# Attention woven step by step into the projections, with 8 slots for stacked heads and 2 for probabilities

## The chip, the core and the metric

The kernel runs on one core of one Trainium2 chip. The metric is the device time of one execution in microseconds (us), as the median of several runs. A core has five engines that run side by side and wait for one another through semaphores: TensorE (PE: matrix products and transposes into PSUM), VectorE (DVE), ScalarE (ACT), GpSimd (POOL) and SyncE (SP), whose queue issues all DMA transfers here. Each engine works through its own instructions in a fixed order.

## What is computed

Two transformer layers over 8 batches of 256 tokens of width 512, in float32. The first is a block with self-attention, cross-attention and an MLP; the second is a recurrent time-mix and channel-mix block, which the change leaves alone. The attention of the first layer, cut to what matters:

```python
def attention(q, k, v, mask):                       # 16 heads of width 32
    scores = einsum('bhqd,bhkd->bhqk', q, k) / sqrt(32)
    scores = scores * mask - 10000.0 * (1.0 - mask)
    return einsum('bhqk,bhkd->bhqd', softmax(scores), v)

h = layernorm(x);  q, k, v = split(h @ w_qkv + b_qkv)
x = x + merge(attention(q, k, v, mask1)) @ w_ao + b_ao
h = layernorm(x);  q = h @ w_q + b_q;  k, v = split(ctx @ w_kv + b_kv)
x = x + merge(attention(q, k, v, mask2)) @ w_co + b_co
x = x + gelu(layernorm(x) @ w1 + b1) @ w2 + b2
```

## The kernel before

**Precision.** Every projection is done on operands that are split into a high and a low part; `mm3` (lines 232 to 234) makes three matmuls of each product. A projection unit of one batch is 48 matmuls of 256 columns for Q or K (`proj_t`, four output quarters of 12 matmuls, in two PSUM banks) or 24 of 512 columns for V and for the output (`proj_n`, two halves of 12).

**Stages of a batch.** The list `jobs` holds 8 batches of self-attention, then 8 of cross-attention, then the MLP. Each job has four stages. Stage `a` loads the input, normalises it (DVE, with a power on GpSimd), transposes it on PE and splits it (ACT, and GpSimd at line 275). Stage `b` makes Q, K and V, and `stack` lays the heads out anew: for each of four groups `hm` it fills a Q tile and a K tile with four DMAs each (line 385), 32 DMAs a batch, in the ring `stk` of six slots. In such a tile the high and low parts of a head lie below each other, so that one matmul makes the whole product of a head. Stage `c` is the attention, stage `d` the output projection and the residual sum (line 348), stored by DMA.

**One head in `attend`.** Two matmuls make the scores `sc` (line 404, two banks). DVE multiplies them by the scaled mask into `e` (line 406, four slots) and takes row minima with the mask's offset (line 408, twice). ACT makes exponentials and their sums (line 411, twice). PE transposes the result with four transposes into `tr` (line 415, two banks), ACT copies it to `pt` (line 419, four slots of two heads). After four heads, eight small products with V fill `cx` (line 424, two banks). After eight heads the reciprocals of the sums are transposed and spread over the partitions (lines 433 to 448), and the context is normalised and split into `ch` and `cl` (lines 449 to 453).

**What sets the order.** The Python loop records stages in the order `c(i)`, `d(i-1)`, `b(i+1)`, `a(i+2)`; this order gives each instruction its priority. A scheduler then puts the instructions of every engine into a fixed order when the program is built, by priority among what it takes to be ready, with a model of its own of how long things take. `tc.high_priority` raises an instruction's priority, and `tc.issue_after(x)` keeps an instruction behind `x` on its engine. Tiles live in named slots of SBUF (`SLOTS`) and PSUM (`BANKS`); a tile that takes a slot waits until the last use of the slot's tile before. Weights, MLP and time-mix follow behind the attention with priorities that are written out by hand (`SEQ`, `AT`).

Of the kernel before, what the change touches and what calls it, by code (L numbers as in the profile page):

```python
# [39 lines left out]
def slots(text):  # L40

    r = {}
    for item in text.split():
# [11 lines left out]
    "attn": slots(  # L55
        "x:a0,a1 xr:a2 y:a3 u:a4-a7 s:a8-a11 v:a12,a13 ch:a14 cl:a15 stk:a16-a21 "
        "w:a16-a23 w1:d1,d3 e:b0-b3 pt:a22-a25 rb:b9 mc:d0,d1 mn:d2,d3 row:b8 sums:c0 mx:c1 rs_:c2 rsp:c3 cp:c4,c6"
    ),
# [47 lines left out]
def block_kernel(ctx: ExitStack, tc: tile.TileContext, a: dict, out: bass.AP):  # L106
# [120 lines left out]

    latest = [None]

    def mm3(o, ah, al, bh, bl, first, last):  # L230
# [77 lines left out]
    def proj_t(w, xt, emit, kind="o", noc=4, pairs=False):  # L308

        (wh, wl), (xh, xl) = w, xt  # L310
        for o2 in range(noc // 2):
            o = bank(kind, [P, 2, T])
            for oo in range(2):
                oc = 2 * o2 + oo
                cs = slice(oc * P, (oc + 1) * P)
                for k in range(KC):
                    mm3(o[:, oo, :], wh[:, k, cs], wl[:, k, cs], xh[:, k, :], xl[:, k, :], k == 0, k == KC - 1)
                if not pairs:
                    emit(oc, o[:, oo, :])
            if pairs:  # L320
                emit(slice(2 * o2, 2 * o2 + 2), o)

    def proj_n(ws, xts, emit, kind="o"):

        for t in range(2):
            ts = slice(t * P, (t + 1) * P)
            o = bank(kind, [P, D])
            n = len(ws)
            for u in range(n):
                (wh, wl), (xh, xl) = ws[u], xts[u]  # L330
                for k in range(KC):
                    mm3(o, xh[:, k, ts], xl[:, k, ts], wh[:, k, :], wl[:, k, :], u == 0 and k == 0, u == n - 1 and k == KC - 1)
            emit(t, o)

# [54 lines left out]
    def attend(qs, ks, v, mc, mn, cp):  # L389
# [3 lines left out]
        lo = wt("cl", [P, KC, T], F32R)  # L393
        for h2 in range(2):
            cx = bank("cx", [P, 2, T])
            sums = wt("sums", [P, 2, 4, 2])
            mx = wt("mx", [P, 2, 4, 2])
            for kk2 in range(2):
                hm = 2 * h2 + kk2
                pts = []  # L400
                for hc in range(4):
                    sc = bank("sc", [P, 2, T])
                    for t in range(2):
                        TE.matmul(sc[:, t, :], qs[hm][:, hc, t * P : (t + 1) * P], ks[hm][:, hc, :], start=True, stop=True)  # L404
                    e = wt("e", [P, 2, T])
                    V.tensor_tensor(e, sc, mc, ALU.mult)  # L406
                    for t in range(2):
                        V.tensor_tensor_reduce(e[:, t, :], e[:, t, :], mn[:, t, :], 1.0, 3.0e38, ALU.add, ALU.min, accum_out=mx[:, kk2, hc, t : t + 1])  # L408
                    pr = e
                    for t in range(2):  # L410
                        S.activation(pr[:, t, :], e[:, t, :], AF.Exp, bias=mx[:, kk2, hc, t : t + 1], scale=-1.0, accum_out=sums[:, kk2, hc, t : t + 1])  # L411
                    pt_ps = bank("tr", [P, 2, T])
                    for kk in range(2):
                        for t in range(2):
                            TE.transpose(pt_ps[:, kk, t * P : (t + 1) * P], pr[:, t, kk * P : (kk + 1) * P], ident)  # L415
                    if hc % 2 == 0:
                        ptt = wt("pt", [P, 2, 2, T])
                    pt = ptt[:, hc % 2]
                    S.copy(pt, pt_ps)  # L419
                    pts.append(pt)  # L420

                def product(kk, hc):
                    h = 4 * hc + hm
                    return TE.matmul(cx[32 * hc : 32 * hc + 32, kk2, :], v[:, kk, 32 * h : 32 * h + 32], pts[hc][:, kk, :], start=kk == 0, stop=kk == 1)  # L424

                with tc.high_priority(1000):
                    first = product(0, 3)
                    with tc.issue_after(first.ins):
                        for kk in range(2):
                            for hc in range(4 if kk else 3):  # L430
                                product(kk, hc)
            rs_ = wt("rs_", [P, 2, 4, 2])
# [3 lines left out]
            V.tensor_copy(rsp[:, :, :, 0, :], rs3)  # L436
            V.tensor_tensor(rsp[:, :, :, 1, :], rs3, r32(rsp[:, :, :, 0, :]), ALU.subtract)
            rt_ps = bank("tr", [8, 2, T])
            for kk in range(2):
                for t in range(2):  # L440
                    TE.transpose(rt_ps[:, kk, t * P : (t + 1) * P].bitcast(F32R), rsp[:, t, kk].rearrange("p u m -> p (u m)"), identr)
            rt = wt("e", [8, 2, T], F32R)
            S.copy(rt, rt_ps)
            rb_ps = bank("tr", [P, 2, T])
            for kk in range(2):
                TE.matmul(rb_ps[:, kk, :], pick, rt[:, kk, :], start=True, stop=True)
            cn = wt("rb", [P, 2, T])
            S.copy(cn, rb_ps)
            V.tensor_tensor(cn, cx, cn, ALU.mult)
            for kk in range(2):  # L450
                k = 2 * h2 + kk
                S.activation(hi[:, k, :], cn[:, kk, :], AF.Identity, bias=cp[:, k : k + 1])
                V.scalar_tensor_tensor(lo[:, k, :], cn[:, kk, :], cp[:, k : k + 1], r32(hi[:, k, :]), ALU.add, ALU.subtract)
        return hi, lo

# [10 lines left out]
    class SelfAttention:  # L466
# [9 lines left out]

        def b(self, b, xt):
            q = qk_t(W[0, "q"], xt, "bqkv", 0)
            k = qk_t(W[0, "k"], xt, "bqkv", 4)
# [3 lines left out]
        def c(self, b, got):  # L483
# [3 lines left out]
            s, v = got  # L487
            return attend(*s, v, *W["mask"], W[0, "cp"])

# [7 lines left out]
    class CrossAttention:  # L497
        slots = "attn"

        def a(self, b, _):  # L500
            if b == 0:
                W[1, "k"] = load_unit(a["wkv"][:, 0:D], "w1")
                W[1, "v"] = load_unit(a["wkv"][:, D : 2 * D], "w1")
                W[1, "q"] = load_unit(a["wq"], "w1")
            et = split_t(load_x(a["ctx"][b], "x"), "u")
            return et, ln_t(load_x(x1[b], "x"), "ln2s", "ln2b")

        def b(self, b, got):
            et, xt = got
            mask = mask_terms(a["cmask"][b, 0])  # L510
            k = qk_t(W[1, "k"], et, "bkv", 0)
            v = v_n(W[1, "v"], et)
            q = qk_t(W[1, "q"], xt, "bq", 0)
            return mask, stack(q, k), v

        def c(self, b, got):
# [3 lines left out]
            mask, s, v = got  # L520
            return attend(*s, v, *mask, W[1, "cp"])

# [549 lines left out]
    def run(ph, stage, b, key):  # L1072
        phase[0] = ph.slots
        got[key] = getattr(ph, stage)(b, got.get(key))


    seq = SEQ.split()
# [19 lines left out]
    for i in range(-2, len(jobs) + 1):  # L1097
        for stage, j in (("c", i), ("d", i - 1), ("b", i + 1), ("a", i + 2)):
            if 0 <= j < len(jobs):
                ph, b = jobs[j]  # L1100
                run(ph, stage, b, j)
        if i >= len(jobs) - 2:
# [54 lines left out]
```

## Time and profile before

| | us |
|---|---|
| median of 3 runs | 1851.51 |
| lowest and highest run | 1848.45, 1852.3 |
| the profiled execution | 1852.05 |
| its span | 1850.1 |
| PE, DVE, ACT, POOL busy in the span | 1691.5, 1313.8, 1152.7, 722.1 |
| first and last scores (line 404) | 53.5, 787.6 |

The profile is one execution. Busy time of PE counts a matmul from its start to its modelled end, and matmuls overlap, so a busy PE is not PE at its peak; the distance between the starts of matmuls tells their price. The granted clock is the share of full speed that PE was given in a stretch. A wait is shown with who ended it, its total, how many there were and the longest.

### The profile page before, as it was taken

Reading aid. Unit: us, or ns where it says so; the run is one execution under the profiler, and the core shown is the slowest. Engines: PE = TensorE matmul, PEld = TensorE weight load, DVE = VectorE, ACT = ScalarE, POOL = GpSimd, SP = SyncE. Lnnn points to the kernel's source line nnn. Section 1 sums busy time; section 2 is a strip of 40 time slices with the busy share of each in tenths; the row PEclk is TensorE's granted clock in tenths of the full one; section 3 lists DMA queues with packets and bytes.
Section 4 is the critical chain, followed back from the end, with each engine's and each line's share of the span. In section 5 each row is a group of like instructions: output and inputs, shape, how many; then the busy total and the mean of one; then the engine's idle time right before and its main releaser. Section 6 shows DMA issues by size and latency. Waiting matters only on the chain.

```text
span 1850.1 us, 38996 instructions
## 1 busy us (share of the span) xinstructions
PE 1691.5 (91%) x14576; PEld 1416.9 (77%) x14576; DVE 1313.8 (71%) x3065; ACT 1152.7 (62%) x2848; POOL 722.1 (39%) x494
## 2 busy tenths in 40 slices
PE   4999999989999999889999999989899998988997
PEld 3777777777778787679999877768788776767876
DVE  4777767787787868864632768876676778799774
ACT  3777777778687868884544454636636453745643
POOL 2011111122222212122211049999999549997000
PEclk9999999999999999999999999999999899889999
DMA  6655545455655655889643555597675848954431
GB/s 188 154 130 127 124 119 130 125 166 150 158 143 143 154 131 139 263 298 330 219 159 107 204 186 165 136 286 222 189 253 172 237 122 254 318 183 141 125 112 48
DMA packets 261026, 324.45 MB, mean 175 GB/s; under 512 B 159155, under 2 KB 162107, under 8 KB 260838
## 3 DMA queue, kind: packets, MB, share of 16 engines
q1 hardware_dynamic: 260838, 321.96, 58.9%
q8 instruction: 116, 1.90, 0.4%
q14 instruction: 72, 0.59, 0.1%
HBM read 156.98 MB, written 97.78 MB: 138 GB/s over the span
## 4 chain that ended last, share of the span: by engine, by line
PE 59%; DVE 15%; DMA 8%; ACT 7%; POOL 5%; issue 4%; SPq 2%; DVEq 0%; ACTq 0%; POOLq 0%
PE o L232 8%; PE o L233 7%; PE o L234 7%; PE mm L232 5%; PE mm L233 5%; PE mm L234 5%; PE tr L415 4%; PE cx L424 3%; PE sc L404 2%; POOL X L848 2%; DVE e L408 2%; DVE e L406 2%; PE out L234 2%; PE out L232 2%; PE out L233 2%
## 5 line engine op out<-in xcount | busy, mean ns | idle before, releaser
L411 ACT ACTIVATE e<-e,mx 128x256 f32<-128x256 f32 x512 | 256.9, 506 | 42.7 <-DVE mx L408 42.1
L406 DVE TENSOR_TENSOR e<-sc,mc 128x512 f32<-128x512 f32 x256 | 171.6, 681 | 99.2 <-PE sc L404 52.7
L408 DVE CUSTOM_DVE_ANT_0 e<-e,mn 128x256 f32<-128x256 f32 x512 | 222.3, 475 | 1.0
L848 POOL TENSOR_TENSOR X<-A,in 128x128 f32<-128x128 f32 (+14 forms) x120 | 208.4, 1780 | 17.8 <-DVE ob L855 13.4
L275 POOL TENSOR_TENSOR u<-y,u 128x1024 fp32r<-128x1024 f32 x32 | 77.7, 2429 | 324.6 <-ACT u L274 268.3
L415 PE MATMUL tr<-ident,e 128*128 128x128 f32 x1024 | 172.7, 284 | 20.7 <-ACT e L411 13.7
L419 ACT COPY pt<-tr 128x512 f32<-128x512 f32 x256 | 147.6, 582 | 30.1 <-PE tr L415 29.5
L232 PE MATMUL mm<-u,whi 128*128 128x256 f32 x512 | 153.3, 300 | 13.0 <-DVE s L368 6.7
L415 PEld LDWEIGHTS tr<-ident,e 128*128 128x128 f32 x1024 | 121.1, 143 | 51.7 <-ACT e L411 22.7
L233 PE MATMUL mm<-u,whi 128*128 128x256 f32 x512 | 147.8, 289 | 4.0 <-POOL u L275 4.0
L232 PE MATMUL o<-u,whi 128*128 128x256 f32 x512 | 146.5, 287 | 1.4 <-DVE xr L348 0.9
L234 PE MATMUL mm<-u,wlo 128*128 128x256 f32 x512 | 147.3, 288 | 0.0
L234 PE MATMUL o<-u,wlo 128*128 128x256 f32 x512 | 145.6, 286 | 0.5 <-DVE wlo L212 0.5
L232 PE MATMUL o<-whi,s 128*128 128x512 f32 x312 | 134.3, 430 | 12.1 <-ACT n L764 4.2
L233 PE MATMUL o<-u,whi 128*128 128x256 f32 x512 | 145.4, 285 | 0.0
L245 POOL TENSOR_TENSOR rstd<-rstd,nhalf 128x2 f32<-128x2 f32 x48 | 35.6, 743 | 261.8 <-DVE rstd L244 252.4
L404 PE MATMUL sc<-stk 128*128 128x256 f32 x512 | 116.6, 320 | 19.2 <-DVE e L406 13.8
L233 PE MATMUL o<-wlo,s 128*128 128x512 f32 x312 | 129.1, 414 | 0.0
L234 PE MATMUL o<-whi,s 128*128 128x512 f32 x312 | 128.8, 414 | 0.0
L830 POOL TENSOR_TENSOR X<-in 128x1024 f32<-128x1024 f32 x48 | 113.5, 2389 | 4.3 <-DVE A L836 4.3
L232 PEld LDWEIGHTS mm<-u,whi 128*128 128x128 f32 x512 | 99.6, 195 | 19.1 <-DVE s L368 8.9
L404 PEld LDWEIGHTS sc<-stk 128*128 128x128 f32 x512 | 82.0, 198 | 40.0 <-DVE e L406 22.8
(358 smaller groups left out, 5056.5 us busy)
## 6 DMA issues: line engine op xcount, KB each, us to landing
stk<-s SPq DMA_DIRECT2D x512, 128.0 KB
x<-x SPq DMA_DIRECT2D x56, 512.0 KB
x<-xr SPq DMA_DIRECT2D x16, 512.0 KB
w<-in_w SPq DMA_DIRECT2D x16, 512.0 KB
w_hi<-whi SPq DMA_DIRECT2D x16, 512.0 KB
w_lo<-wlo SPq DMA_DIRECT2D x16, 512.0 KB
w<-v SPq DMA_DIRECT2D x32, 256.0 KB
whi<-w_hi SPq DMA_DIRECT2D x16, 512.0 KB
```

The costliest lines, as they stand in the source:

```text
L232: TE.matmul(o, ah, bh, start=first, stop=False)
L233: TE.matmul(o, ah, bl, start=False, stop=False)
L234: latest[0] = TE.matmul(o, al, bh, start=False, stop=last)
L275: (eng or V).tensor_tensor(lo, y, r32(hi), ALU.subtract)
L404: TE.matmul(sc[:, t, :], qs[hm][:, hc, t * P : (t + 1) * P], ks[hm][:, hc, :], start=True, stop=True)
L406: V.tensor_tensor(e, sc, mc, ALU.mult)
L408: V.tensor_tensor_reduce(e[:, t, :], e[:, t, :], mn[:, t, :], 1.0, 3.0e38, ALU.add, ALU.min, accum_out=mx[:, kk2, hc, t : t + 1])
L411: S.activation(pr[:, t, :], e[:, t, :], AF.Exp, bias=mx[:, kk2, hc, t : t + 1], scale=-1.0, accum_out=sums[:, kk2, hc, t : t + 1])
L415: TE.transpose(pt_ps[:, kk, t * P : (t + 1) * P], pr[:, t, kk * P : (kk + 1) * P], ident)
L419: S.copy(pt, pt_ps)
L830: G.tensor_tensor(X.rearrange("p (i s d) -> p i s d", i=ni, s=m), rb[:, t0 : t0 + ni, :].unsqueeze(2).broadcast_to([P, ni, m, 64]), kb[:, ...
L848: G.tensor_tensor(Y.rearrange("p (h j s) -> p h j s", h=4, j=16), A[:, t, 0:n, :].rearrange("p s h -> p h s").unsqueeze(2).broadcast_to([P ...
```

## The change

Attention becomes a generator of 20 steps a batch. Step `at` issues the scores of head `at` and the transposes of head `at - 2`; every fourth step issues the context of four heads; steps 9 and 17 the reciprocals, 10 and 18 their transposes, 11 and 19 the normalisation. `weave` starts a batch's chain with its first step, and `tick`, called behind each of the four quarters of a Q or K unit and each of the four quarters of a V or output unit, runs one more step of every chain that is open. Four units make 16 ticks, so the last three steps of a chain run with the first steps of the next batch's. The PE instructions of a step are kept behind the last projection matmul that was recorded before them (`after`).

Stage `b` is cut in two: `q` makes Q of batch i + 1 ahead of the output projection of batch i - 1, and K, V and the stacking stay in `b`. In cross-attention the transposes of the context input become a stage of their own (`e`), V comes after K and the stacking, and the weights of Q are loaded first. The ring of stacked heads grows from six slots to eight, the whole of a batch; the slots come from `pt`, which keeps two of four. Sums and minima get a tile for each half of the heads.

In the diff below, the bodies of the functions inside `attend` are those of the loop before.

```diff
-... stk:a16-a21 ... pt:a22-a25 ... sums:c0 mx:c1 rs_:c2 rsp:c3 cp:c4,c6
+... stk:a16-a23 ... pt:a24,a25 ... sums0:c0 mx0:c1 sums1:c4 mx1:c5 rs_:c2 rsp:c3 cp:c7,c6
...
+    woven, done = [], []
+    def tick():
+        for step in list(woven):
+            step()
+    def after():
+        return nullcontext() if latest[0] is None else tc.issue_after(latest[0].ins)
...
     # proj_t, behind the 12 matmuls of a quarter
+                tick()
...
     # proj_n, behind 6 matmuls
+                    if k % 2:
+                        tick()
...
     # attend
+        halves = [(bank("cx", [P, 2, T]), wt(f"sums{h2}", [P, 2, 4, 2]), wt(f"mx{h2}", [P, 2, 4, 2])) for h2 in range(2)]
+        def scores(h): ...          # matmuls under after(); e, minima, exponentials
+        def transposed(h): ...      # transposes under after(); copy to pt
+        def context(hm): ...        # first product under high_priority(1000) and after(), the others behind it
+        def reciprocals(h2): ...
+        def rows(h2): ...
+        def normed(h2): ...
+        for at in range(20):
+            if at % 4 == 2 and at > 2:
+                context(at // 4 - 1)
+            if at in (11, 19):
+                normed((at - 11) // 8)
+            if at in (10, 18):
+                rows((at - 10) // 8)
+            if 2 <= at < 18:
+                transposed(at - 2)
+                if at in (9, 17):
+                    reciprocals((at - 9) // 8)
+            if at < 16:
+                scores(at)
+            if at < 19:
+                yield
...
     # SelfAttention; CrossAttention likewise
+        def q(self, b, xt):
+            return xt, qk_t(W[0, "q"], xt, "bqkv", 0)
-        def b(self, b, xt):
-            q = qk_t(W[0, "q"], xt, "bqkv", 0)
+        def b(self, b, got):
+            xt, q = got
...
-            return attend(*s, v, *W["mask"], W[0, "cp"])
+            return (yield from attend(*s, v, *W["mask"], W[0, "cp"]))
...
+    def weave(j):
+        ph, b = jobs[j]
+        steps = ph.c(b, got[j])
+        while woven and done[-1] < 17:
+            woven[0]()
+        done.append(0)
+        def step():
+            phase[0] = ph.slots
+            done[j] += 1
+            try:
+                next(steps)
+            except StopIteration as end:
+                got[j] = end.value
+                woven.remove(step)
+        woven.append(step)
+        step()
...
     for i in range(-2, len(jobs) + 1):
-        for stage, j in (("c", i), ("d", i - 1), ("b", i + 1), ("a", i + 2)):
-            if 0 <= j < len(jobs):
-                ph, b = jobs[j]
-                run(ph, stage, b, j)
+        if 0 <= i < 2 * NB:
+            weave(i)
+        todo = [("q", i + 1), ("d", i - 1), ("a", i + 2), ("b", i + 1), ("e", i + 2)]
+        if i + 2 >= 2 * NB:
+            todo = ([("c", i)] if i >= 2 * NB else []) + [("q", i + 1), ("d", i - 1), ("b", i + 1), ("all", 0), ("a", i + 2)]
+        for stage, j in todo:
+            if stage == "all":
+                while i >= 2 * NB - 1 and woven:
+                    tick()
+            elif 0 <= j < len(jobs) and hasattr(jobs[j][0], stage):
+                while stage == "d" and j == i - 1 and len(woven) > (0 <= i < 2 * NB):
+                    woven[0]()
+                run(jobs[j][0], stage, jobs[j][1], j)
```

## The prediction, made before the changed kernel was run

> **What bounds the kernel now.** I read the page first: its engine shares and the chain that ended last.
>
> ```profile
> span 1850.1 us, 38996 instructions
> PE 1691.5 (91%) x14576; PEld 1416.9 (77%) x14576; DVE 1313.8 (71%) x3065; ACT 1152.7 (62%) x2848; POOL 722.1 (39%) x494
> PE 59%; DVE 15%; DMA 8%; ACT 7%; POOL 5%; issue 4%; SPq 2%; DVEq 0%; ACTq 0%; POOLq 0%
> ```
>
> TensorE is the bound, but over a third of the chain runs through others. The changed code lies between the first and last scores, 53 to 808 us: 16 batches, some 47 us apart. So I asked next for the table by stages.
>
> ```profile
> core 0: us, PE busy (x) PEld busy (x) DVE busy (x) ACT busy (x) POOL busy (x), PEclk, DMA share, GB/s
> 180.00:192.00 12.00, 9.69 (x71) 7.44 (x69) 9.06 (x23) 8.82 (x23) 2.50 (x1) 0.99 0.80 191
> 192.00:204.00 12.00, 11.14 (x64) 8.44 (x65) 10.16 (x34) 8.69 (x28) 0.80 (x1) 0.73 0.05 12
> 204.00:216.00 12.00, 12.00 (x110) 10.98 (x109) 8.50 (x33) 8.83 (x27) 2.52 (x2) 1.00 0.51 143
> 216.00:228.00 12.00, 11.83 (x88) 9.96 (x87) 6.10 (x23) 8.89 (x28) 0.00 (x0) 1.00 0.65 145
> 53.00:808.00 755.00, 695.52 (x5226) 570.82 (x5224) 567.81 (x1781) 596.16 (x1695) 120.66 (x82) 0.98 0.57 149
> ```
>
> The first four rows are one batch: one slice with 2.3 us of idle PE, the next at a granted clock of 0.73 with almost as few instructions, then two full slices. In all, PE is idle 755.0 - 695.5 = 59.5 us. The waits of PE in that stage say for whom:
>
> ```profile
> PE sc L404 <- DVE e L406: 13.8, 19, 2.4
> PE tr L415 <- ACT e L411: 13.7, 20, 1.6
> PE tr L415 <- ACT pt L419: 6.6, 8, 3.1
> PE sc L404 <- DMA stk<-s: 4.5, 4, 1.7
> PE cx L424 <- ACT pt L419: 3.3, 9, 0.8
> ```
>
> It is the softmax chain: scores wait for a bank that DVE must read, transposes for exponentials. Yet DVE (567.8) and ACT (596.2) are busy only three quarters of the stage. The timeline of that batch shows why both hold:
>
> ```profile
> 182.01 0.69 DVE L406 TENSOR_TENSOR e<-sc,mc 128x512 f32<-128x512 f32 x1 [6.18 <-PE sc L404]
> ...
> 187.45 2.59 DVE L408 CUSTOM_DVE_ANT_0 e<-e,mn 128x256 f32<-128x256 f32 x1
> ...
> 190.74 0.55 PE L415 MATMUL tr<-ident,e 128*128 128x128 f32 x3 [1.60 <-ACT e L411]
> ```
>
> DVE stood 6.18 us without scores while PE worked through the V projection; then heads came in a burst, one minimum took 2.59 us instead of 0.41 (GpSimd's 2.50 us low part, L275, ran beside it from 187.26), and PE ran dry.
>
> **What one batch costs PE at full pace.** A busy matmul of 0.28 us is not its price, since they overlap; the distance between starts is:
>
> ```profile
> 208.59 0.28 PE L232 MATMUL mm<-u,whi 128*128 128x256 f32 x1
> 208.71 0.28 PE L233 MATMUL mm<-u,whi 128*128 128x256 f32 x1
> ...
> 213.69 0.60 PE L415 MATMUL tr<-ident,e 128*128 128x128 f32 x4
> 214.05 0.36 PE L232 MATMUL mm<-u,whi 128*128 128x256 f32 x1
> ```
>
> So 0.118 us for a 256-wide matmul and, read the same way, 0.233 for a 512-wide one, 0.28 for a head's two scores, 0.45 for its four transposes with the switch, 1.1 for a context, 0.4 for four LayerNorm transposes. Over the stage: about 1540 x 0.118 + 746 x 0.233 + 256 x (0.28 + 0.45) + 64 x 1.1 + 46 for the rest (19 LayerNorm, 27 normalising) = 182 + 174 + 187 + 70 + 46 = about 659 us. The stage lasts 96 us longer: 59.5 idle, (1 - 0.98) x 755 = 15 of lowered clock, 21 counted busy in drained pipelines.
>
> **The change, part by part.**
>
> No arithmetic is added: same scores, transposes, products and copies, and the 512 stacking DMAs. What moves is the order, which I took from the two built programs, pricing the PE work between two instructions with the distances above.
>
> *Spreading the heads.* Before, the output projection's 24 matmuls (5.6 us) hold nine heads; with their transposes and a context PE has 13 us of work there, ACT 9 x 1.5 = 13.5 us (0.49 an exponential, 0.5 a copy) before its other work; no scores come during most of the V unit. After, the same 24 matmuls hold four heads, 10.6 us of PE against some 7 of ACT, and 16 heads spread over 37 to 41 us of PE work instead of 29 to 37. Scores whose bank was filled less than 2 us of PE work earlier (two score banks, as before): 50 heads before, 16 after. Heads, outside the first and last batch, whose transposes come under 4.5 us of PE work behind their scores: 27 before, 14 after. The bare chain takes about 3.2 us (multiply 0.6, two minima 0.7, exponentials 1.0, score drain and hand-overs the rest), 2.2 more where GpSimd's pass meets it. Idle by waits falls to between a third and a half. From 725 to 810, PE is idle 11.8 us; that last batch has nothing to weave into in either order, so I leave it. Of 59.5 - 11.8 = 47.7 us, 24 to 32 go; I take 30, since before the tight heads came four or five in a row and after come singly. Bounds: 0, if the waits only change place, and 47.7.
>
> *Clock.* The lowered slices follow the idle ones, so they go with them: of 15 us (some 3 in the last batch), I take 11; bounds 0 and 15. The Trainium skill, "TensorE: Matmul & The Clock Gate", section "HAM oscillation — how this bites in real kernels", asks only that PE have no idle gap over about 3.4 us. Here the clock fell to 0.73 behind gaps of 1.60 and 1.30 us, and no wait in this stage is over 3.1. By the page this term would be 0 and the forecast 11 us later; I go by the row.
>
> *Drains counted busy.* They belong to the same waits; of 21 us I take 9, because switching between matmul kinds stays. Bounds 0 and 21.
>
> The same page ("A second HAM failure mode: psum-queue depth-cycling") speaks against this change: small groups cycling through few banks make PE pause and the clock oscillate. The row from 204 to 216, where quarters of 12 matmuls alternate with scores and transposes, has PE busy 12.00 of 12.00 at clock 1.00. By the page the gain would shrink to the idle term; the row decides.
>
> *Eight stacking slots.* Before, a batch's last pair of stacks had to wait for its own first heads; now it waits for heads 12 to 15 of the batch before. The four DMA waits of scores (4.5 us) lie in the idle term.
>
> *Two probability slots instead of four.* A context must end before the next copy may write: ACT waits for PE, and exponentials stand behind it on ACT. The order puts a context 1.4 to 3.4 us of PE work behind the last transposes, where drain and copy (0.27 + 0.58) need about 1. Cost 0 to 0.2 us a batch.
>
> *Queries ahead of the chain's end.* Q of batch i+2 is now evicted right after head 15 of batch i, and its buffers come free when the last four stacks of Q(i+1) have left; those wait for head 15's scores. Cover: 0.4 + 1.1 + 0.9 + 0.4 + 0.28 + 1.42 = 4.5 us of PE work. Need: four issues x 0.588 = 2.4 plus a landing of 2.2 to 4.1 (pieces of the chain that ended last). ACT's eviction is 0.1 to 2 us late, exponentials behind it; most is covered by the 5 us before those transposes. With the two slots I take 3 us in sum; bounds 0 and 14 x 2.2 = 31.
>
> *Other queues.* On SP a store of the output projection now stands within the Q stacks, and two loads behind it; the next stacks are needed a quarter of a batch later. GpSimd's and DVE's other work is unchanged. Start, MLP and time-mix: same order as before but for a few instructions; GpSimd's busy stretch there starts earlier by whatever attention saves, so I carry it through whole.
>
> Sum: 30 + 11 + 9 - 3 = 47 us. The profiled execution took 1852.05 us, 1.95 around the span and 0.5 over the median: 1852.05 - 47 - 0.5 = 1804.5 us.
>
> **The rivals.**
>
> *More comes back (0.13).* Nearly all of 47.7, 12 and 14: 74 us less, 1778, down to 1768. For it: ACT and DVE have a quarter of the stage free. Against it: 14 tight heads remain, and GpSimd still stretches DVE once a batch.
>
> *Waits change place (0.15).* A third of the idle time, no clock, 4 of drains: 16 + 4 - 3 = 17 us, 1834; up to 1846. For it: ACT and DVE near 85% of a 42 us batch, in fixed order. Against: fewer heads close together.
>
> *The Q stacks decide, slower (0.11).* If one 512 KB transfer lies in front of the last Q stacks (5.2 us in two pieces of the chain), ACT's eviction is up to 7 us late; if PE sees 5 of them in 14 batches, 70 us go: 1851.5 - 50 (the three gains) + 70 = about 1872. It decides from 3.6 us a batch (50 / 14) on. Against: in the order those transfers stand behind the last stacks or well ahead of them.
>
> *No change (0.01)*: PE's sequence is another, so only by accident.
>
> **How the numbers follow.** The main case has 0.60, 1782 to 1826. With the rivals' ends down to 1768 and up to 1843 the range leaves out 0.2. A difference under 0.2% (3.7 us) can't be told from none. Faster: 0.60 + 0.13 + 0.13 of the third case = 0.86; same 0.03; slower 0.11.
>
> **What would show it.** The stage from the first to the last scores should take 707 us or so instead of 755, with some 30 us of idle PE, at most two or three lowered clock windows, batches 44 us apart, and DVE's long idle during V gone. The waits of scores for DVE and of transposes for ACT should halve. Wrong would be a new large wait of ACT's eviction of s for DMA stk, of the copy to pt for PE, or an unchanged stage with the gain lost behind 808 us.

## The result, and the profile after

The changed kernel takes 1900.31 us (median of 4 runs, 1896.62 to 1902.64), the kernel before 1851.9 beside it: 1.025 times as long, 95% interval 1.0226 to 1.0273. The forecast was 1804.5 us. The profiled execution took 1900.18 us, its span is 1898.4.

The page of the changed kernel, engine shares and the chain that ended last:

```profile
PE 1708.7 (90%) x14576; PEld 1425.1 (75%) x14576; DVE 1334.6 (70%) x3065; ACT 1156.7 (61%) x2850; POOL 724.0 (38%) x494
PE 54%; DVE 14%; DMA 12%; POOL 8%; ACT 7%; issue 3%; SPq 2%; ACTq 0%; DVEq 0%; POOLq 0%
```

The same 14576 matmuls, more time in them, and DMA has gone from 8% of the chain to 12%. To find the 48.3 us of span I cut both executions at the start of the last normalisation of the context (the multiply into `rb`), which closes a batch's attention: first batch, the 14 batches between, last batch. The table by stages of the kernel before, then of the changed one:

```profile
53.00:102.00 49.00, 44.96 (x346) 37.27 (x344) 40.57 (x128) 42.02 (x122) 6.30 (x4) 0.98 0.66 155
102.00:750.40 648.40, 604.55 (x4570) 498.91 (x4570) 484.27 (x1541) 502.43 (x1455) 106.76 (x71) 0.98 0.54 138
750.40:809.00 58.60, 46.91 (x319) 35.18 (x318) 43.06 (x115) 52.41 (x121) 7.59 (x7) 0.94 0.81 273
```

```profile
57.00:115.60 58.60, 51.93 (x367) 43.00 (x367) 39.25 (x135) 40.31 (x119) 3.96 (x3) 0.91 0.57 133
115.60:787.00 671.40, 616.63 (x4549) 497.80 (x4547) 498.58 (x1549) 511.28 (x1472) 109.50 (x72) 0.97 0.56 143
787.00:844.60 57.60, 45.85 (x298) 34.35 (x298) 32.58 (x99) 45.58 (x105) 6.20 (x7) 0.86 0.45 162
```

The first batch closes 13.6 us later (115.6 against 102.0), the 14 batches take 23.0 longer (671.4, 648.4), the last one 1.0 less, and what lies behind the attention 12.6 longer (1053.8 to the end of the span, 1041.2 before): 48.3 in all. PE's idle time in the 14 batches went from 43.9 to 54.8 us, the clock from 0.98 to 0.97. The waits of PE in the stage (57 to 845 us) say what became of the chain:

```profile
PE mm L242 <- DVE s L381: 28.0, 17, 6.3
PE mm L242 <- ACT ch L485: 11.9, 10, 4.4
PE sc L417 <- DVE e L419: 7.7, 8, 4.9
PE tr L432 <- ACT e L423: 6.7, 11, 1.9
PE cx L444 <- ACT pt L435: 5.4, 3, 2.6
PE tr L432 <- ACT pt L435: 2.9, 6, 1.6
```

Scores waiting for DVE (`sc`) and transposes waiting for ACT (`tr`, two lines) are the waits that the change was to shorten: 13.8, 13.7 and 6.6 us before, about half of that now. Most of what is left lies in the first and the last batch: in the 14 batches between, scores wait 1.6 us for DVE (13.4 before) and transposes 1.6 for exponentials (9.0). The context's wait for `pt` grew, 3.3 to 5.4. The first two lines are new. The projections, which never waited for long, now wait 28.0 us for DVE's eviction of Q and K (`s`, which frees their PSUM bank), and the output projection, straight behind the chain's end, 11.9 us for ACT. The timeline of one such wait, rows of SP's queue, GpSimd, DVE and PE:

```profile
219.95 0.54 SPq L353 DMA_DIRECT2D x<-in_x  x1
...
222.34 2.35 POOL L285 TENSOR_TENSOR u<-y,u 128x1024 fp32r<-128x1024 f32 x1 [34.40 <-ACT u L284]
...
223.86 1.29 DVE L251 BATCH_NORM_STATS2 st<-x 128x6 f32<-128x512 f32 x2 [1.79 <-DMA x<-in_x]
...
225.43 0.48 DVE L381 SCALAR_TENSOR_TENSOR s<-mm,cv,s 128x256 fp32r<-128x256 f32 x1
...
225.97 0.39 PE L242 MATMUL mm<-u,whi 128*128 128x256 f32 x1 [3.14 <-DVE s L381]
```

SP issues the load of x for a LayerNorm at 219.95. DVE is free for its statistics at 222.07 and stands 1.79 us; the statistics take 1.29 more, and behind them in DVE's fixed order is the eviction that PE needs: 3.14 us without a matmul. In the stage DVE stands 24.0 us so, 14 times (17.5 us for `x` made by the kernel, 6.5 for the input); before, it was 6.2 us (4.7 and 1.5). In the changed list the LayerNorm (stage `a`) is recorded ahead of K and V; it was the last stage of a batch before.

### The profile page after: what moved, and what is told of

Same layout as the page of the kernel before. It is cut to its first block, busy times and chain, and to the rows that moved or that the text cites. A ratio compares the mean times of both kernels' runs of the same rounds, so it can differ in the third digit from the quotient of the medians.

```text
span 1898.4 us, 38990 instructions
## 1 busy us (share of the span) xinstructions
PE 1708.7 (90%) x14576; PEld 1425.1 (75%) x14576; DVE 1334.6 (70%) x3065; ACT 1156.7 (61%) x2850; POOL 724.0 (38%) x494
## 4 chain that ended last, share of the span: by engine, by line
PE 54%; DVE 14%; DMA 12%; POOL 8%; ACT 7%; issue 3%; SPq 2%; ACTq 0%; DVEq 0%; POOLq 0%
PE o L242 6%; PE o L243 6%; PE o L244 6%; PE mm L242 5%; PE mm L243 5%; PE mm L244 5%; PE tr L432 4%; PE cx L444 3%; DMA x<-x 3%; POOL X L888 2%; PE sc L417 2%; PE out L242 2%; PE out L244 2%; PE out L243 2%; DVE e L419 2%
## 5 line engine op out<-in xcount | busy, mean ns | idle before, releaser
L421 DVE CUSTOM_DVE_ANT_0 e<-e,mn 128x256 f32<-128x256 f32 x512 | 211.7, 455 | 2.3
L242 PE MATMUL mm<-u,whi 128*128 128x256 f32 x512 | 156.7, 306 | 41.0 <-DVE s L381 34.4
L432 PE MATMUL tr<-ident,e 128*128 128x128 f32 x1024 | 162.2, 282 | 11.4 <-ACT e L423 6.7
L243 PE MATMUL mm<-u,whi 128*128 128x256 f32 x512 | 149.8, 293 | 4.0 <-POOL u L285 4.0
L242 PE MATMUL o<-whi,s 128*128 128x512 f32 x312 | 131.4, 421 | 15.8 <-DVE n L797 4.6
L242 PEld LDWEIGHTS mm<-u,whi 128*128 128x128 f32 x512 | 102.5, 200 | 47.9 <-DVE s L381 38.1
L244 PE MATMUL o<-whi,s 128*128 128x512 f32 x312 | 126.2, 405 | 0.0
L243 PEld LDWEIGHTS mm<-u,whi 128*128 128x128 f32 x512 | 102.6, 200 | 4.5 <-POOL u L285 4.3
```

The source lines that it names most:

```text
L242: TE.matmul(o, ah, bh, start=first, stop=False)
L243: TE.matmul(o, ah, bl, start=False, stop=False)
L244: latest[0] = TE.matmul(o, al, bh, start=False, stop=last)
L432: TE.transpose(pt_ps[:, kk, t * P : (t + 1) * P], e[:, t, kk * P : (kk + 1) * P], ident)
```

## The experiments

Theories: **A**, the LayerNorm's new place makes K's evictions late (A1, by its load; A2, by its own work on DVE and GpSimd). **B**, the hand-written order (`after()`) costs by itself. **C**, the two ends of the stage. **D**, two probability slots. **E**, part of the loss is no part of the change: the scheduler deals what lies behind the attention anew. All runs in one table, from the traces, cut as above; "pause" is the time from the start of DVE's last gradient-step tile `ob` of the time-mix's fifth batch to that of its first of the sixth (the expectation of e14 gives 85 and 100 us for the kernel before and e5; by these marks it is 82 and 99). The medians are of 3 to 10 runs, but the stages are those of one execution: 14 runs of the kernel before on one chip lay between 1846.9 and 1861.9 us, and the profiled run of e11 is 8 us faster and that of e18 6 us slower than the median.

| kernel | median us | first batch ends | 14 batches | last | from there to the end | pause |
|---|---|---|---|---|---|---|
| before | 1851.5 | 102.0 | 648.4 | 58.5 | 1041.2 | 82 |
| after | 1900.3 | 115.6 | 671.4 | 57.6 | 1053.8 | 98 |
| e1 loads on GpSimd's queue | 1913.7 | 116.8 | 683.5 | 56.8 | 1055.7 | 101 |
| e2 no `after()` | 1893.6 | 103.5 | 666.3 | 51.3 | 1071.6 | 115 |
| e3 plain ends | 1893.4 | 106.2 | 675.4 | 47.9 | 1061.8 | 106 |
| e4 before, slots alone | 1892.4 | 102.6 | 648.5 | 63.8 | 1078.8 | 111 |
| e5 before, `pt` rotated | 1862.9 | 101.0 | 650.5 | 62.4 | 1049.1 | 99 |
| e6 LayerNorm behind K | 1861.7 | 109.2 | 637.0 | 62.1 | 1056.4 | 105 |
| e7 LayerNorm ahead of output projection | 1901.4 | 119.0 | 659.7 | 60.4 | 1060.4 | 88 |
| e8 e2 + e3 | 1877.8 | 104.6 | 648.2 | 51.3 | 1070.6 | 113 |
| e9 loads recorded early | 1905.3 | 111.9 | 670.3 | 59.9 | 1066.7 | 98 |
| e10 e3 + e6 | 1869.4 | 100.2 | 644.5 | 47.7 | 1076.5 | 111 |
| e11 e3 + e6 + early loads | 1860.7 | 97.0 | 650.4 | 47.9 | 1055.6 | 104 |
| e12 e2 + e3 + e6 | 1860.6 | 99.9 | 627.4 | 54.0 | 1079.2 | 116 |
| e13 LayerNorm without its load | 1906.7 | 114.3 | 659.6 | 58.6 | 1080.0 | 112 |
| e14 before, `stk` rotated | 1876.0 | 101.6 | 650.9 | 62.8 | 1060.9 | 108 |
| e15 e12, `stk` rotated | 1850.1 | 99.6 | 625.3 | 50.4 | 1070.8 | 112 |
| e16 e12, `s` rotated | 1853.0 | 99.8 | 624.8 | 53.3 | 1073.5 | 106 |
| e17 e15, second MLP one earlier | 1838.9 | 99.8 | 628.8 | 51.8 | 1057.0 | 99 |
| e18 e15, second MLP two earlier | 1855.3 | 99.6 | 630.9 | 50.7 | 1078.1 | 115 |

**e1, loads on another queue.**

```diff
 def load_x(src, tag):
-    nc.sync.dma_start(out=x, in_=tok(src))
+    (nc.gpsimd if phase[0] == "attn" and tag == "x" else nc.sync).dma_start(out=x, in_=tok(src))
```

> The changed kernel with one thing moved: the loads of x for the LayerNorms and of the encoder states in the attention go out on GpSimd's DMA queue instead of SP's, so that they stand behind no stacking DMA and no store of the output projection. The trace of the changed kernel shows DVE standing 24.0 us at the first statistics of a LayerNorm for such a load (17.5 and 6.5 us, 14 times; 6.2 us before the change), with the evictions of s queued behind it, and PE waiting 28.0 us for those evictions. Theory A (the late loads hold DVE's queue, and they are what eats the gain): both waits go to a few us and the time falls by 20 to 30 us, to 1870 to 1880. Rival B (the order written out by hand is the cost, whatever the loads do): the wait of DVE goes but PE waits for something else, and the time stays within 8 us of 1900. Rival C (the two ends of the stage are the cost): within 12 us of 1900, and the first and last batch as long as they were.

Slower than the changed kernel: 1913.7. DVE's wait for x rose to 35.8 us and PE's for `s` to 38.4, so the loads came still later. The edit didn't bring about what it was made for, and by itself says nothing against A; that the two waits rose together speaks for it.

**e2, no `after()`.**

```diff
 def after():
-    return nullcontext() if latest[0] is None else tc.issue_after(latest[0].ins)
+    return nullcontext()
```

> The changed kernel without the constraints that hold each step's PE instructions behind the last matmul of the projection quarter before it: the steps are recorded in the same places, but the scheduler may put heads earlier or later. Theory A (late loads): the loads stand where they stood, so the time stays at 1885 to 1905. Rival B (the fixed order costs): the time falls to near the kernel before, 1845 to 1865. Rival C (ends): the first batch no longer waits for the units of the next one, so its 15 us come back, and perhaps the last one's 11 to 17 us: 1870 to 1885.

The first batch gets 12 us back and the last one 6, the 14 batches only 5, and the end loses 18 more. PE's wait for `s` falls to 15.4 us, while scores wait for DVE 23.0. B's 1845 to 1865 missed.

**e3, plain ends.** First and last chain are recorded in one go, without `after()`.

```diff
     def after():
-        return nullcontext() if latest[0] is None else ...
+        return nullcontext() if latest[0] is None or plain[0] else ...
     # weave
+        while woven and j == 2 * NB - 1:
+            woven[0]()
...
+        plain[0] = j in (0, 2 * NB - 1)
         step()
+        while plain[0] and step in woven:
+            step()
+        plain[0] = False
```

> The changed kernel with the first and the last attention batch not woven: their 20 steps are recorded in one go and without the constraints, as before the change; the 14 batches between stay as changed. By the distance at equal PE work the first two batches lost 15 us, the last one 11 to 17, the batches between 8 to 10. Theory C (the ends): 20 to 30 us less, 1870 to 1880. Theory A (late loads) and rival B (order): at most 10 us less, since 14 of 16 batches are as they were.

Both ends are 10 us shorter (106.2, 47.9), so C holds for them. The 14 batches took 4 and the end 8 more, so the time shows 7 and C's 1870 to 1880 was missed.

**e4, the slots alone**, on the kernel before.

```diff
-stk:a16-a21 ... pt:a22-a25
+stk:a16-a23 ... pt:a24,a25
```

> The kernel before with nothing but the changed buffers: eight slots for stacked heads and two for probabilities; order and code as before. Theory D (two probability slots cost: the copies wait for contexts, 31.0 us of ACT in the changed kernel, exponentials behind them): 10 to 30 us slower than before, 1860 to 1880. Theories A, B and C: within 5 us of 1851.5; eight stacking slots may give back 4 us of waits.

The time, 1892.4, is above theory D's range, and not for its reason: the 14 batches take 648.5 against 648.4 us, the first and the last together 6 more, and 38 us are lost behind the attention. That part of the program has no line changed; what is another is the scheduler's order of it, and which slots are shared with the attention's tiles. This run gave rise to theory E.

**e5 and e14, two controls for E**, on the kernel before: the same slots in another rotation.

```diff
-pt:a22-a25
+pt:a23,a24,a25,a22     # e5
-stk:a16-a21
+stk:a17-a21,a16        # e14
```

> A control on the kernel before: its four probability slots are handed out in another rotation (a23, a24, a25, a22 instead of a22 to a25). No work, no slot count and no dependence inside the attention changes, and each engine's order is that of the kernel before up to the last attention batch; behind it the scheduler deals the instructions of last batch, MLP, time-mix and channel-mix anew. Theory E (part of the loss is not the change at all: the kernel before has an unusually good order behind the attention, and any edit that makes the scheduler deal it anew loses it; 13 of the 48 us of the changed kernel lie behind 1133, up to 37 in the run with the slots alone): 15 to 35 us slower than before, the attention up to 740 us as long as before to 2 us. Without theory E: within 5 us of 1851.5.

> A second control on the kernel before: the six slots of the stacked heads handed out in another rotation. Nothing changes up to the middle of the last attention batch, behind which the scheduler deals the instructions anew. Theory E: 5 to 30 us slower than before, all of it behind the attention, and with a longer pause of the time-mix between its fifth and sixth batch (85 us from the last gradient-step tile ob of one to the first of the next in the kernel before, 100 in the first control). Without theory E: within 5 us.

No work is added or left out, and they are slower by 10 us (1.0064, interval 1.0039 to 1.0089) and 23 us (1.0124, 1.0093 to 1.0155). E holds, though e5 stayed under the 15 us that it was given. The 14 batches moved by 2 us, the last batch by 4; the end by 8 and 20, with the pause 17 and 26 us longer. In the traces the order on PE, DVE and ACT is that of the kernel before up to 806 us (e5) and 784 us (e14) and another one behind; so the 2 us of the 14 batches, where the order is the same, are the spread from one execution to another. A rotation also changes which tile of the attention a later tile in the same slot has to wait for; the runs don't part this from the order. Every other kernel in the table has an end of 1049 us or more, the kernel before 1041: what a change saves in the attention is set against the best of twenty deals.

**e6, the LayerNorm behind K.** `b` is cut in two (`b`: K and stacking, `v`: V).

```diff
-todo = [("q", i + 1), ("d", i - 1), ("a", i + 2), ("b", i + 1), ("e", i + 2)]
+todo = [("q", i + 1), ("d", i - 1), ("b", i + 1), ("a", i + 2), ("v", i + 1), ("e", i + 2)]
```

> The changed kernel with the LayerNorm of batch i+2 recorded between the K and the V projection of batch i+1 instead of between output projection and K (projections, heads and the loads' queue as changed): DVE's queue then has the statistics behind the evictions of K, and the load has some 10 us more to land. The run with the loads on GpSimd's queue did not settle theory A, since the loads came later still there (35.8 us of DVE waits for them, and PE's wait for the evictions of s rose with them, 28.0 to 38.4 us). Theory A (a LayerNorm load that is late holds DVE's queue, with the evictions behind it): DVE's wait for x falls from 24.0 to under 6 us, PE's wait for s from 28.0 to under 10, the time to 1870 to 1885. Rival B (the order written by hand costs by itself, 24 of 35 us went with its constraints in the run without them): PE's wait for s stays above 20 us whatever the loads do, and the time within 8 us of 1900.

39 us faster than the changed kernel, more than A gave it: 1861.7. The 14 batches take 637.0, 34 less than after and 11 less than before. PE's waits in them (109 to 746 us), largest four:

```profile
PE mm L242 <- DVE mv L252: 15.1, 7, 3.4
PE mm L242 <- DVE s L381: 7.6, 9, 2.6
PE mm L242 <- ACT ch L485: 5.0, 8, 0.8
PE tr L432 <- ACT pt L435: 3.1, 3, 1.6
```

Scores waiting for DVE and transposes waiting for exponentials (13.4 and 9.0 us in these batches before) are no longer among them. DVE's waits for x fell from 24.0 to 7.9 us (A had under 6), PE's for `s` from 28.0 to 11.8 in the stage (A had under 10). The 15.1 us behind the LayerNorm's aggregate (`mv`) are seven waits, all in cross-attention, and still DVE's queue. The longest:

```profile
453.64 1.29 DVE L251 BATCH_NORM_STATS2 st<-x 128x6 f32<-128x512 f32 x2 [1.78 <-DMA x<-x]
...
456.26 0.55 PE L242 MATMUL mm<-u,whi 128*128 128x256 f32 x1 [3.37 <-DVE mv L252]
```

The statistics of a LayerNorm stand 1.78 us for x. Behind them on DVE comes, at 455.43, the pass that makes the low part `u` of the context input out of a PSUM bank; it ends at 456.11, and the projection's matmul starts at 456.26. So the projections' waits for DVE, 26.8 us in the 14 batches of the changed kernel, are still 22.7 here. What else fell shows in the row of this stage:

```profile
109.00:746.00 637.00, 599.57 (x4553) 496.07 (x4551) 488.69 (x1542) 508.88 (x1470) 109.37 (x72) 0.98 0.58 147
```

Of the 34 us, 17 are PE's idle time (54.8 to 37.4) and 17 its busy time (616.6 to 599.6), in which lowered clock (0.97 to 0.98) and drained pipelines count.

**e7, the LayerNorm earlier still.**

```diff
-todo = [("q", i + 1), ("d", i - 1), ("a", i + 2), ("b", i + 1), ...
+todo = [("q", i + 1), ("a", i + 2), ("d", i - 1), ("b", i + 1), ...
```

> The changed kernel with the LayerNorm of batch i+2 recorded ahead of the output projection of batch i-1 instead of behind it, so that four transposes stand between the end of a chain and the projection that reads it. PE waits there 11.9 us in the changed kernel (mm for ch, ten times). If that wait is a cost of its own, 5 to 10 us less, 1890 to 1895. By theory A the statistics now stand still earlier in DVE's queue than the load can land: DVE's waits for x rise above 30 us, PE's for s above 30, and the time is 1900 to 1915.

The time is that of theory A, its reason isn't: DVE waits only 6.3 us for x, and PE 9.0 for `s`. PE waits for other things instead (14.7 us for `cl`, 11.4 for exponentials). A late load isn't needed for the loss; that opened A1 against A2.

**e8, no `after()` and plain ends.**

> Both of the partial repairs together: no constraints that tie the steps to the quarters, and first and last batch recorded in one go. At the first MLP matmuls the changed kernel stands 35 us behind the kernel before, the run without constraints 11, the run with plain ends 21. If these are two causes that add, this one stands within 3 us of the kernel before there; if the constraints are the common cause, at 8 to 13 us behind. By theory E the end is 13 to 35 us later again than that, so 1865 to 1890 in all; without it, 1851 to 1865.

The last context is normalised 5 us ahead of the kernel before and 40 ahead of the changed kernel, where e2 and e3 by themselves gain 23 and 15, so at this mark the two add up. Column by column they don't: the 14 batches take 5 us less in e2, 4 more in e3 and 23 less here, with the LayerNorm where the change put it. The end took 1070.6, as E said, and the time was 1877.8.

**e9 and e13, A1 against A2.** e9 records the load of batch i+3 behind the LayerNorm of batch i+2. e13 makes the LayerNorms from the Q weights and doesn't load x, except in the first batch of each phase.

```diff
-[("a", i + 2), ("b", i + 1), ("e", i + 2)]
+[("a", i + 2), ("l", i + 3), ("b", i + 1), ("e", i + 2)]     # e9; l: x = load_x(...)
...
-    V.bn_stats(st[:, t, :], x[:, t, :])
+    V.bn_stats(st[:, t, :], (x if stats[0] is None else r32(stats[0]))[:, t, :])     # e13
```

> The changed kernel with the load of x for the LayerNorm of batch i+3 recorded behind the LayerNorm of batch i+2, on SP as before: the load has a batch to land, and the LayerNorm stays where the change put it, ahead of K. It parts two readings of the run with the later LayerNorm, which got 39 us back. Theory A1 (it was the load: DVE stood for x with the evictions of s behind it): DVE's wait for x goes below 8 us, PE's wait for s from 28.0 to about 10, and the time to 1860 to 1875. Theory A2 (it is the place of the LayerNorm's own work on DVE, ACT and GpSimd, between output projection and K): DVE's wait goes but the time stays at 1885 to 1905, as in the run with the output projection later, where DVE's waits for x were small, 6.3 us, and the time 1901.

> The changed kernel with the attention's LayerNorms (all but the first of each phase) computed from the Q weights in place of x, which is then not loaded: the LayerNorm does the same work in the same recorded place but waits for no transfer. Theory A1 (the load is what costs): PE's wait for s falls from 28.0 us to about 10 and the time by 20 us or more, to 1860 to 1880. Theory A2 (the place of the LayerNorm's work): the wait of DVE for x is gone, but PE's waits for evictions stay above 20 us in all and the time is 1885 to 1905.

e9 settled nothing: DVE still waits 29.5 us, because the scheduler moved the statistics along with the load (load at 214.40 us, statistics wanted at 217.4; 219.95 and 222.1 in the changed kernel). e13 is the test. Its time, 1906.7, is that of A2, but 26 us of it are a longer end. In the 14 batches, 659.6 us, 12 of the 34 us are gone; PE's wait for `s` is 21.2 us, 28.0 in the changed kernel. So the load is about a third of it and the LayerNorm's own place the rest (e13 also moves fewer bytes and deals the order anew, so the third is a rough share). Rows of e13 show one way in which the second part comes about (its line numbers are one higher than those above):

```profile
599.21 0.42 DVE L422 CUSTOM_DVE_ANT_0 e<-e,mn 128x256 f32<-128x256 f32 x1
599.41 2.43 POOL L286 TENSOR_TENSOR u<-y,u 128x1024 fp32r<-128x1024 f32 x1
599.56 2.58 DVE L422 CUSTOM_DVE_ANT_0 e<-e,mn 128x256 f32<-128x256 f32 x1
...
602.55 0.48 DVE L382 SCALAR_TENSOR_TENSOR s<-mm,cv,s 128x256 fp32r<-128x256 f32 x1
...
603.09 0.38 PE L243 MATMUL mm<-u,whi 128*128 128x256 f32 x1 [2.35 <-DVE s L382]
```

GpSimd's low part of a LayerNorm (2.43 us) runs beside one minimum of a head, which takes 2.58 us instead of 0.42. K's eviction stands behind it on DVE, and PE waits 2.35 us. Counted over the 14 batches, PE's gaps of 0.3 us and more that fall beside such a pass or within 1.5 us behind it are 14.0 us in the changed kernel, 26.9 in e7, 30.2 in e2 and 4.2 in e6. But they are 12.3 us in the kernel before too, so these passes don't explain why the changed kernel is slower than it. Why they are few in e6 is argued, not shown: V is evicted by ACT's copies alone, so beside V no bank hangs on DVE's queue.

**e10, e11, e12, the repairs together.** e10 is e3 and e6; e11 has the early loads of e9 as well; e12 is e10 without `after()`.

> The later LayerNorm and the plain first and last batch together, a candidate that may beat both kernels. At the MLP's first matmuls the later LayerNorm stands level with the kernel before (12 us ahead until the last batch, which gives them back, and 7 us lost in the first). If the ends are a cause that adds to the LayerNorm's place, this one stands 10 to 18 us ahead there, and if the end of the kernel loses the same 10 us as in the control with rotated slots, the time is 1842 to 1852. If the ends had only the same cause as the batches between: level there, 1858 to 1868.

> As the run before it, with the loads of x recorded a batch early as well. With the later LayerNorm DVE still waits 8.0 us for x and PE 15.1 us for evictions behind the LayerNorm's aggregate. Theory A1: most of these go, and the 14 batches between take another 8 to 15 us less: 1830 to 1845. Theory A2: within 5 us of the run without the early loads.

> The later LayerNorm and plain ends, without the constraints that tie the steps to the quarters. Rival B (the hand-written order costs by itself): faster than the run with them by 10 us or more. If the constraints only hurt because the LayerNorm stood in the wrong place (the scheduler could put heads between when it was free to): no faster, and scores wait for DVE again, 15 to 23 us instead of 4, as in the two runs without constraints.

In the attention they gain: the last context is normalised 17 us (e10), 14 (e11) and 28 (e12) ahead of the kernel before. e11 against e10 settles nothing between A1 and A2: DVE's wait for x hardly changed (7.1 to 5.4 us in the stage), PE waits 7.2 us for the context input's loads, and the 14 batches take 6 us more. The time, 1860.7, is 9 us below e10's, by a shorter end, and in neither theory's range. e10's 1842 to 1852 was missed too, with the place in the attention as forecast. e12 against e10 is B: 627.4 against 644.5 us, so with the LayerNorm in its place the constraints cost 17 us in the 14 batches, and the scores' waits for DVE, which I had thought would come back without them, are 4.9 us in the stage. But the times, 1869.4, 1860.7 and 1860.6, are all above the kernel before, since the ends are 1055.6 to 1079.2.

Read at the last context (the first three columns added up), the runs part three causes. The LayerNorm's place is worth 36 us in the changed kernel (844.6 to 808.3, e6), 37 with plain ends (829.5 to 792.5, e3 to e10) and 23 with plain ends and no constraints (804.1 to 781.2, e8 to e12). The constraints are worth 23, 25 and 11 us (after to e2, e3 to e8, e10 to e12): with plain ends each of the two is worth 14 us less when the other is gone. Plain ends are worth 15 to 17 us (after to e3, e2 to e8, e6 to e10).

**e15 to e18, the end dealt anew.**

```diff
-stk:a16-a23
+stk:a17-a23,a16                                # e15, e17, e18; e16: s:a9-a11,a8 instead
-"f": 2.5, "h": 4.7, "i": 5.5, "j": 7.7,
+"f": 1.5, "h": 3.7, "i": 4.5, "j": 6.7,        # e17; e18: one less again
```

> The kernel without constraints, with the later LayerNorm and plain ends (28 us ahead of the kernel before at the MLP, 1861 at the end), with the eight stacking slots in another rotation: the attention the same, the end dealt anew. Theory E: the end moves by up to 20 us either way, 1840 to 1880, with the attention within 3 us of what it was. Otherwise 1860 within 4 us.

> As the run before, with the rotation of the four buffers of s changed instead. Theory E: 1840 to 1880 again, and another time than the run before; otherwise 1860 within 4 us.

> The best kernel so far (no constraints, later LayerNorm, plain ends, rotated stacking slots) with the second pass of the MLP (batches 5 to 7) given a priority one batch earlier among the time-mix. If its pause between the fifth and sixth batch of the time-mix (112 us) is that pass being late, the pause shrinks by 10 to 25 us and the time to 1825 to 1840. If TensorE has no room for it earlier anyway, the first five batches of the time-mix get longer by what the pause loses, and the time stays at 1845 to 1855.

> As the run before, two batches earlier. Same alternatives: 1820 to 1840 with a shorter pause, or 1845 to 1860 with longer batches ahead of it.

The deal alone moves e12's 1860.6 to 1850.1 (0.9978 of the kernel before, 0.996 to 0.9997) and 1853.0 (0.9998, 0.9979 to 1.0017). e17 takes 1838.9 us and beats both kernels, the one before by under 1%: 0.9915, interval 0.9884 to 0.9946, with a pause of 99 us. e18 has a pause of 115 and no gain (1.0001, 0.9977 to 1.0025), so it isn't simply that the second MLP was late. The 14 batches of e17, by stage and by PE's largest waits:

```profile
99.78:728.60 628.82, 599.50 (x4581) 498.48 (x4579) 500.57 (x1564) 512.45 (x1483) 110.12 (x73) 0.98 0.59 151
```

```profile
PE mm L276 <- ACT v L389: 6.1, 6, 1.2
PE cx L445 <- ACT pt L436: 4.9, 9, 0.7
PE tr L480 <- ACT e L472: 4.6, 2, 4.2
PE mm L276 <- DVE s L382: 3.0, 3, 2.1
```

PE is idle 29.3 us there, against 43.9 before and 54.8 after, and no line of its waits for DVE is over 3.0 us in sum.

## Why the prediction was wrong

**Spreading the heads: right in its mechanism, too large in its size.** In the 14 batches scores' waits for DVE fell from 13.4 to 1.6 us and transposes' for exponentials from 9.0 to 1.6; over the stage they halved. But what that is worth with nothing new in the way is seen in e15 to e17: 20 to 24 us less in the 14 batches, 14.6 of it idle time in e17, where the sum had 47 us for the stage. Batches were to be 44 us apart; those of e17 are 44.9 (628.8 / 14), of the changed kernel 48.0. The stage of 53 to 808 us that the prediction calls first to last scores ends with the last normalisation (the last scores are at 787.6); in the changed kernel it takes 788 us (57 to 845), where the forecast was 707. The rival in which waits change place had this part of the picture, but had it faster than before (1834).

**Clock and drains: wrong in the changed kernel, and too large without its new waits.** The clock of the 14 batches fell to 0.97, that of the first batch to 0.91 and of the last to 0.86. Where the new waits are gone it is 0.99 (e12, e15, e16) or 0.98 (e17), 0.98 before, and PE's busy time in the 14 batches is 5 to 9 us less (595.2 to 599.5, 604.5 before). The sum had 11 + 9 = 20 us for the two in the whole stage: the right sign, two to four times the size. The Trainium skill, "TensorE: Matmul & The Clock Gate", section "A second HAM failure mode: psum-queue depth-cycling", tells of a bf16 kernel of 512 columns that cycled through PSUM banks and whose clock oscillated; it gives no size of a group. In e17 groups of 12 matmuls alternate with heads too, at a mean clock of 0.98, which agrees with the row that the prediction went by.

**Slots: right as far as shown.** e4's 14 batches are 0.1 us apart from the kernel before, in the order of before. In the changed order a sign of being wrong that the prediction named did appear: ACT's copy to `pt` waits 31.0 us for PE's contexts (no such wait before, 11.1 us in e6, 1.8 in e12). No run gives the changed order more than two slots, so what this costs there isn't shown. **Queries ahead of the chain's end: right.** ACT's eviction of `s` waits 4.1 us in all for the stacks, 1.9 before; the sum had 3 with the slots. The rival with this mechanism, at 1872, had the sign and not the cause.

**Other queues: the step that failed.** It followed two loads on SP past the next stacks and found them not needed until later. It didn't follow the LayerNorm that one of these loads feeds: stage `a` was moved ahead of K on DVE, ACT and GpSimd, and "GpSimd's and DVE's other work is unchanged" held for its amount and not for its place. The sum had nothing for it. In its place the runs showed waits of PE for the evictions of Q and K of 25.9 us in the 14 batches, 2.3 before; with the stage put back behind K, these 14 batches take 34 us less and the kernel 39, and with the LayerNorm where it was but its load left out, about a third of the 34 is gone. How the rest is lost is shown only in part: half of the 34 us is PE's busy time, and in e6 waits behind the LayerNorm's aggregate take the place of most of those for `s`. The diff's list of stages says so in one line, and the row of the 2.59 us minimum, shown in the prediction itself, pointed at DVE's queue.

**What was not in the sum.** The output projection waits 11.9 us for `ch`: it stands straight behind the chain's end. The constraints were taken as the order one wants; they cost 11 to 25 us up to the last context. Without them PE's largest wait of e10, 14.5 us behind the LayerNorm's aggregate, is gone (e12); that PE goes on to other work that is ready is inferred. And "the same order as before but for a few instructions" failed at the start, 13.6 us, of which plain ends alone give back 9.5 (e3).

**"Carry it through whole": wrong.** Behind the attention 12.6 us were lost, and edits that change no work lose 8 and 20 there. That step would have failed with a faster attention too: e12, 28 us ahead at its last context, took 1.002 times the time before (1.000 to 1.004). The range should have had the spread of the end, 8 to 39 us by the table, and on one side only.

**Open.** How the two thirds of the LayerNorm's place that aren't its load divide between GpSimd's passes, the mere order on DVE and PE's longer busy time; why the constraints are worth 5 us in the 14 batches with woven ends (e2) and 27 with plain ones (e3 to e8); why the first batch hangs on the ticks as it does; and which instruction of the end makes the pause 82 us in one deal and 116 in another.

## What to carry to other kernels

When a stage changes its place in a recorded order, follow each of its instructions on each in-order engine and ask who stands behind it: a LayerNorm that nobody waits for, recorded ahead of a projection instead of behind it, cost 39 us here, in part because evictions that free a PSUM bank stood behind its statistics. Before crediting or blaming a change in a scheduled program, run one or two edits that change no work (a rotated slot list); here they moved the time by 10 and 23 us, a fifth and a half of what the change cost. Compare stage by stage at fixed landmarks, since a real gain of 28 us in one stage can be hidden by another stage's order.

## What the runs showed of the hardware

PE's clock fell behind short gaps. In the changed kernel's first batch PE waits 1.43 us for an exponential (up to 61.05 us) and 1.94 us for an eviction (up to 64.03), and by windows of 4 us:

```profile
60.00:64.00 4.00, 0.88 (x4) 0.45 (x4) 2.31 (x11) 3.78 (x14) 0.00 (x0) 0.87 0.91 204
64.00:68.00 4.00, 3.97 (x18) 3.98 (x19) 0.85 (x2) 0.63 (x2) 0.00 (x0) 0.50 0.58 174
```

The clock is 0.50 in the four microseconds behind them, with PE busy 3.97 of 4.00. The Trainium skill, "TensorE: Matmul & The Clock Gate", section "HAM oscillation — how this bites in real kernels", gives the rule of no idle gaps of PE over about 3.4 us. Here the clock fell behind two shorter ones with a microsecond of work between them, 3.37 us together. That the gaps are the reason is inferred from what came first; no run varies them alone.
